# Mixer: seven products of values of cubics for each square or triangle of four filter blocks, and a table for the remainder's taps

## The chip, the cores and the metric

The kernel runs on one NeuronCore of a Trainium2 chip. Five engines work beside each other, each on its own list of instructions in order: PE (TensorE) multiplies matrices into PSUM, DVE (VectorE), ACT (ScalarE) and POOL (GpSimd) do elementwise work, and SP (SyncE) issues DMAs here. They wait for one another by semaphores. The metric is the time of one execution on the device in microseconds (us).

## The reference

Four layers follow one another on an image of 2 x 56 x 56 tokens with 128 channels: two layers of selective scans, then attention plus a spectral mixer, then attention plus a mixture of experts. The change lies in the mixer of the third layer alone. Cut to what matters, it computes this from the layer-normed tokens `u` (2 x 3136 x 128), 16 filters `phi`, and `s = sigma ** 0.25`:

```python
# U_plus: causal convolution of u with each phi[:, k]
# U_minus: the same with u's sign alternating in time, and the sign put back after
out = einsum('btkd,k,kde->bte', U_plus, s, M_phi_plus)
out = out + einsum('btkd,k,kde->bte', U_minus, s, M_phi_minus)
out = out + sum(einsum('btd,de->bte', shifted(u, i), M_u[i]) for i in range(3))
```

It does so for the first T, T/2, T/4 and T/8 tokens with four sets of matrices, and adds the four with the weights of a softmax. The convolution is causal, so the four can share it: which matrices apply depends only on the stretch in which an output token lies.

## The kernel before

Alternating the sign of `u` in time only changes the sign of products between an even and an odd position. So the kernel splits tokens and taps into even and odd ones, of length `HL` = 1568, convolves each parity of the input (`pin`) with each parity of the taps (`eo`), and uses the sum or the difference of the two matrices (`both`) afterwards. A convolution is a lower triangular Toeplitz matrix in blocks of `KB` = 128: `NB` = 12 blocks and a rest of `REST` = 32.

`mixer_filters` prepares the taps. It loads the padded filters into `P`, writes them to DRAM as `raw`, forms 23 sums of blocks of filters on DVE (L1480), and writes them to DRAM as `win`. It runs inside the start of the third layer's attention (`Attention2.run`), and DVE's next instruction after it is the `skip` matrix of the attention (L1286), which its first scores need. During the attention `MixerInputs` lays out the tokens: even ones into the SBUF tile `x`, odd ones through small tiles `r` (two buffers) into the DRAM tile `odd`.

`layer2_mixer` is one stage of 32 units: the parity of the input is the outer loop, then pairs of filters `f0`, then `eo`. Two units with the same pair of filters are called a pair here. In a unit, `H` and the windows `wA` to `wD` hold the Toeplitz matrices, loaded by SP a unit or more ahead. The twelve output blocks are three groups of four: `u0` (a triangle of taps on the first blocks), the two halves of `u1`, and a shared part `S`. The tables `TRIANGLE` and `SQUARE` name each product: which blocks of filters are summed, which combination of inputs stands against it, and to which output blocks it is added. A triangle takes 8 products, a square 9.

`product` (matmuls at L1690) makes one product as 128x256 matmuls for each of two batches, into one of six PSUM buffers `cv`. `into` takes it out: ACT copies the first one for a block (L1705), DVE adds the others to their blocks (L1703), and the sum of S and D (L1707). POOL adds `S` to the second half of `u1` (L1734). `project` multiplies a finished tile with the matrices `Wm` (L1804, two PSUM buffers `pj`), and DVE adds to the output `A` (L1810). `remainder` (L1752) does the last 32 positions for both parities of taps, in units with eo=0.

The order of every engine is the order in which the program is written: `u0`, then the projection of the last unit's `u1` and rest (`finish`), the two halves of `u1`, `S`, `D`, the projection of `u0`, the remainder. Once per pair `matrices` loads `mpm` for two filters, POOL forms `both` (L1784, L1785), DVE the weighted sums `Wm` (L1838, L1840 in `stretch_sums`). Once per parity `inputs` forms the combinations of inputs on DVE (L1619 and the lines after it). Elsewhere, L1840 also serves `MixerInputs`, and L1049 is POOL's end of the second layer.

Of the kernel before, what the change touches and what calls it, by code (L numbers as in the profile page):

```python
# [14 lines left out]
F32 = mybir.dt.float32  # L15
# [6 lines left out]
B = 2  # L22
HW = 56
L = HW * HW
C = 128
# [1384 lines left out]
def key_tiles(k, ps, uT, V, c):  # L1410
# [26 lines left out]
TRIANGLE = (  # L1437
    ((0,), "t3", (3,)), ((3,), "x0", (3,)), ((1,), "t2", (2,)), ((2,), "t1", (1,)), ((0,), "x0", (0,)),
    ((0, 1), "x2", (3, 2)), ((0, 2), "x1", (3, 1)), ((1, 2), "x0", (2, 1)),
)  # L1440
SQUARE = (
    ((0,), "a0", (3,)), ((1,), "a1", (2,)), ((2,), "h0", (1,)), ((3,), "h1", (0,)),
    ((0, 1), "a01", (3, 2)), ((2, 3), "h01", (1, 0)), ((0, 2), "m0", (3, 1)), ((1, 3), "m1", (2, 0)),
    ((0, 1, 2, 3), "m01", (3, 2, 1, 0)),
)


def filter_sums():


    def sums(table, *bases):
        return [tuple(sorted(b + i for i in f for b in bases)) for f, _, _ in table if len(f) * len(bases) > 1]

    first = sums(SQUARE, 0) + [(1, 2)]
    return {"A": first, "B": sums(TRIANGLE, 8), "C": sums(SQUARE, 0, 4), "D": sums(SQUARE, 4)}


SUMS = filter_sums()
NWIN = sum(len(v) for v in SUMS.values())
# [3 lines left out]
def mixer_filters(k, d, dp):  # L1463


    nc = k.nc
    raw = dp.tile([32, PW], F32, name="raw")
    win = dp.tile([32, NWIN, WIDE], F32, name="win")
    with k.tc.tile_pool(name="m2f", bufs=1) as fp:
        P = fp.tile([32, PW], F32, name="P")  # L1470
        nc.gpsimd.memset(P, 0.0)
        nc.sync.dma_start(P[:, KB - TP : KB + HL], d["L2_phi"].rearrange("f p m -> (f p) m"))
        nc.sync.dma_start(raw, P)
        D = fp.tile([32, NWIN, WIDE], F32, name="D")
        done = {(i,): P[:, KB * i + 1 : KB * i + 1 + WIDE] for i in range(NB)}
        at = 0
        for group in SUMS.values():
            for f in sorted(group, key=len):
                two = next((a, b) for a in done for b in done if tuple(sorted(a + b)) == f)
                nc.vector.tensor_tensor(D[:, at + group.index(f)], done[two[0]], done[two[1]], ALU.add)  # L1480
                done[f] = D[:, at + group.index(f)]
            at += len(group)
        nc.sync.dma_start(win, D)
    return raw, win
# [105 lines left out]
class Mixer:  # L1590
# [5 lines left out]

    def __init__(self, k, ctx, given, raw, win):
        self.k, self.x, self.odd, self.raw, self.win = k, given.x, given.odd, raw, win  # L1600
        sp = ctx.enter_context(k.pool("mixv", 1))
        self.wp = ctx.enter_context(k.pool("mixw", 1))
        self.cp = ctx.enter_context(k.pool("mixc", 1))
        self.p1 = ctx.enter_context(k.pool("pconv", 6, psum=True))
        self.sp = sp
        self.H = self.wp.tile([KB, 2, 2, HL], F32, name="H")
        self.W, self.waiting = {}, None

    def inputs(self, par):

        nc, x = self.k.nc, self.x
        if par:
            for j in (8, 4, 0, NB):
                js = slice(j, min(j + 4, NB + 1)) if j == NB else slice(j, j + 4)
                nc.sync.dma_start(x[:, js], self.odd[:, js])
        self.v = {f"x{i}": x[:, NB - 1 - i, :] for i in range(NB)}

        def less(out, a, b):
            nc.vector.tensor_tensor(out, a, b, ALU.subtract)  # L1619

        t = self.sp.tile([KB, 3, B * C], F32, name="t")
        x0, x1, x2, x3 = (self.v[f"x{i}"] for i in range(4))
        nc.vector.scalar_tensor_tensor(t[:, 0], x1, -1.0, x0, ALU.mult, ALU.subtract)
        less(t[:, 1], x1, x2)
        less(t[:, 1], t[:, 1], x0)
        less(t[:, 2], x3, x2)
        less(t[:, 2], t[:, 2], x1)
        self.v |= {f"t{i + 1}": t[:, i] for i in range(3)}

        def twice(v):  # L1630
            return v.unsqueeze(1).to_broadcast([KB, 2, B * C])

        for name in "ACD":

            c = self.scratch("S", 7)
            e = self.scratch("u0", 5)
            v = self.sp.tile([KB, 9, B * C], F32, name="v" + name)
            if name == "A":
                less(c, x[:, 0:7], x[:, 4:11])
            elif name == "C":  # L1640
                c = x[:, 4:11]
            else:
                less(c[:, 0:4], x[:, 8:12], x[:, 4:8])
                nc.vector.tensor_scalar_mul(c[:, 4:7], x[:, 8:11], -1.0)
            less(e, c[:, 0:5], c[:, 2:7])
            less(v[:, 0:2], e[:, 0:3:2], twice(e[:, 1]))
            less(v[:, 2:4], twice(e[:, 3]), e[:, 2:5:2])
            less(v[:, 4:6], c[:, 1:6:4], twice(c[:, 3]))
            less(v[:, 6:8], c[:, 2:5:2], twice(c[:, 3]))
            nc.vector.tensor_copy(v[:, 8], c[:, 3])  # L1650
            self.v |= {name + n: v[:, i] for i, n in enumerate(("a0", "a1", "h0", "h1", "a01", "h01", "m0", "m1", "m01"))}

    def scratch(self, name, n):
        t = self.cp.tile([128, B, 2, 4 * KB], F32, name=name).rearrange("p b f c -> p (b f c)")
        return t[:, 0 : n * B * C].rearrange("p (k c) -> p k c", c=B * C)

    def taps(self, f0, eo):

        self.k.nc.sync.dma_start(
            self.H[:, eo],  # L1660
            bass.AP(self.raw.tensor, self.raw.offset + (2 * f0 + eo) * PW + 1, [[1, KB], [2 * PW, 2], [1, HL]]),
        )

    def windows(self, name, f0, eo):
        n, n0 = len(SUMS[name]), sum(len(SUMS[m]) for m in SUMS if m < name)
# [8 lines left out]
    def products(self, table, name, bases, prefix, eo):  # L1674

        by = {}
        for f, v, outs in table:
            key = tuple(sorted(b + i for i in f for b in bases))
            if len(key) == 1:
                h = self.H[:, eo, :, KB * key[0] : KB * (key[0] + 1)]  # L1680
            else:
                h = self.W[name][:, :, SUMS[name].index(key), :]
            by.setdefault(outs, []).append((self.v[prefix + v], h))
        return by

    def product(self, terms):
        ps = self.p1.tile([128, B, 2, KB], F32, name="cv")
        for b in range(B):
            for i, (v, h) in enumerate(terms):
                self.k.nc.tensor.matmul(  # L1690
                    ps[:, b], lhsT=v[:, C * b : C * (b + 1)], rhs=h, start=i == 0, stop=i == len(terms) - 1
# [3 lines left out]
    def into(self, by, place, onto=None):  # L1695
# [3 lines left out]
        for outs in sorted(by, key=len):  # L1699
            ps = self.product(by[outs])  # L1700
            for o in outs:
                if len(outs) > 1:
                    nc.vector.tensor_tensor(place(o), place(o), ps, ALU.add)  # L1703
                elif onto is None:
                    nc.scalar.copy(place(o), ps)  # L1705
                else:
# [468 lines left out]
```

## Time and profile before

| | us |
|---|---|
| median of three runs | 9005.99 (9002.64 to 9015.55) |
| the profiled execution | 9012.54 |
| its span | 9010.8, mean granted TensorE clock 0.954 |
| scan layers, start of the attention | 0 to 5757 |
| `mixer_filters` and start of the attention proper | 5757 to 5780 |
| attention of layer 3 | 5780 to 6390 |
| mixer | 6400.4 to 8069.3 |
| last attention and experts | 8069.3 to 9010 |

Stages are read from the timeline by the lines that belong to them. In the mixer PE is busy for 1652 of 1669 us, DVE for 1141, ACT for 230 and POOL for 230. In the views below, a row of windows gives for a stretch of time the busy us of each engine with the number of instructions, then the granted clock, the share of DMA and GB/s. A row of waits names who waited, for whom, the total, the number and the longest. A row of a group or a line gives the operation, its shape, the count and the duration, and for a source view the smallest, median and largest duration in ns.

### The profile page before, as it was taken

What the parts mean: (1) busy time and instruction counts of PE and PEld (TensorE: products, weight loads), DVE (VectorE), ACT (ScalarE), POOL (GpSimd) and SP (SyncE); (2) the same over time, 40 slices, a digit from 0 to 9 for tenths busy, and PEclk for the clock granted to TensorE, in tenths of its full rate; (3) what the DMA queues carried; (4) which work ended last, traced back from release to release, by engine and by line L of the source; (5) the groups of instructions that cost most, each with busy time, mean ns of one, the idle gap of its engine ahead of it and who ended that gap; (6) DMA issues with size and microseconds to landing.
All of it is one profiled execution on the core that took longest, in us unless ns stands there. A gap on an engine that the chain in (4) does not pass through costs nothing. (4 is left out here: it accounts for less than half of the span.)

```text
span 9010.8 us, 104738 instructions
## 1 busy us (share of the span) xinstructions
PE 8222.8 (91%) x32399; PEld 5096.0 (57%) x32399; DVE 6874.5 (76%) x7312; ACT 5097.6 (57%) x11031; POOL 6021.1 (67%) x3874
## 2 busy tenths in 40 slices
PE   8999989999998888888888888699999999999998
PEld 4555555555554444444445444455688888874555
DVE  8999988999978996997998899421576676665442
ACT  6888877888866775775776777443211111114331
POOL 5999987999977996996998799466311111115551
PEclk9999999999998997998998999799999999999999
DMA  5666654666645873884785687000333333320004
GB/s 149 217 218 212 212 165 148 217 215 212 211 145 156 223 215 108 227 219 114 217 220 150 179 221 214 10 3 3 91 106 99 103 96 105 94 62 8 15 1 136
DMA packets 751756, 1286.57 MB, mean 143 GB/s; under 512 B 129005, under 2 KB 401390, under 8 KB 751162
## 3 DMA queue, kind: packets, MB, share of 16 engines
q1 hardware_dynamic: 751194, 1279.86, 48.6%
q8 instruction: 257, 4.21, 0.2%
q14 instruction: 305, 2.50, 0.1%
HBM read 1239.96 MB, written 39.60 MB: 142 GB/s over the span
## 5 line engine op out<-in xcount | busy, mean ns | idle before, releaser
L492 POOL TENSOR_TENSOR p<-h,c 128x784 f32<-128x784 f32 x2048 | 3763.8, 1863 | 293.8 <-DVE h L401 147.7
L401 DVE TENSOR_TENSOR_SCAN h<-a,state,h 128x784 f32<-128x784 f32 x1200 | 2169.4, 1832 | 2.9 <-ACT a L381 2.3
L421 PE MATMUL acc<-p,center 128*128 128x392 f32 x4096 | 1491.6, 500 | 6.0 <-POOL p L492 5.9
L421 PE MATMUL acc<-p,ident 128*128 128x392 f32 x4096 | 1431.0, 493 | 0.5 <-POOL p L492 0.4
L476 DVE TENSOR_TENSOR h<-du,b 128x784 f32<-128x784 f32 x1152 | 1095.4, 951 | 233.1 <-PE b L407 211.2
L381 ACT ACTIVATE a<-delta,L1A 128x784 f32<-128x784 f32 x896 | 819.8, 915 | 423.4 <-DVE h L401 418.8
L421 PEld LDWEIGHTS acc<-p,ident 128*128 128x128 f32 x4096 | 748.4, 190 | 534.2 <-issue 34.5
L421 PEld LDWEIGHTS acc<-p,center 128*128 128x128 f32 x4096 | 741.8, 193 | 495.3 <-issue 23.5
L1220 POOL TENSOR_TENSOR total<-total,e 128x448 f32<-128x448 f32 (+1 forms) x644 | 734.2, 1140 | 328.8 <-ACT e L1209 289.2
L1703 DVE TENSOR_TENSOR u<-u,cv 128x512 f32<-128x512 f32 x1024 | 623.2, 678 | 326.7 <-PE cv L1690 325.5
L1734 POOL TENSOR_TENSOR u<-u,S 128x1024 f32<-128x1024 f32 x64 | 150.0, 2364 | 1041.2 <-DVE S L1703 1025.8
L495 POOL TENSOR_TENSOR h<-du,b 128x784 f32<-128x784 f32 x448 | 831.7, 1856 | 0.0
L1209 ACT ACTIVATE e<-sc 128x448 f32<-128x448 f32 (+1 forms) x700 | 376.9, 542 | 726.3 <-PE sc L1207 594.1
L407 PE MATMUL b<-three,sel 96*128 96x512 bf16 (+1 forms) x2304 | 587.5, 336 | 181.4 <-DVE h L476 110.2
L381 ACT ACTIVATE a<-delta,L0A 128x784 f32<-128x784 f32 x704 | 643.2, 914 | 170.3 <-DVE h L401 165.6
L401 DVE TENSOR_TENSOR_SCAN h<-a,h 128x784 f32<-128x784 f32 x400 | 702.4, 1773 | 3.4 <-ACT a L381 3.1
L359 ACT ACTIVATE X<-X,BT 112x128 f32<-112x128 f32 x2100 | 683.8, 391 | 0.2
L1705 ACT COPY u<-cv 128x512 f32<-128x512 f32 x256 | 149.3, 586 | 828.2 <-PE cv L1690 774.6
L401 DVE TENSOR_TENSOR_SCAN h<-h,state,a 128x784 f32<-128x784 f32 x336 | 617.6, 1838 | 0.0
L407 PEld LDWEIGHTS <-sel 96*128 96x128 bf16 x2304 | 224.2, 100 | 526.7 <-issue 367.0
L359 ACT ACTIVATE big<-big,BT 112x64 f32<-112x64 f32 x1680 | 444.6, 335 | 0.0
L370 PE MATMUL a<-ident,X 112*128 112x112 f32 x2240 | 292.7, 269 | 83.5 <-DVE h L401 76.2
(485 smaller groups left out, 13801.3 us busy)
## 6 DMA issues: line engine op xcount, KB each, us to landing
c<-rows SPq DMA_DIRECT2D x1024, 392.0 KB, 4.0
c<-rows SPq DMA_DIRECT2D x2048, 196.0 KB, 4.0
b<-rows SPq DMA_DIRECT2D x512, 196.0 KB, 4.4
b<-rows SPq DMA_DIRECT2D x192, 392.0 KB, 4.5
H<-raw SPq DMA_DIRECT2D x32, 1568.0 KB, 6.4
wC<-win SPq DMA_DIRECT2D x64, 576.0 KB, 5.7
w<-in_L_weight_dram SPq DMA_DIRECT2D x52, 512.0 KB, 4.6
wA<-win SPq DMA_DIRECT2D x64, 384.0 KB, 5.4
```

Of the source, the lines that this page charges most:

```text
L359: self.k.nc.scalar.activation(x["bT"][:, i, c0:c1], g["duT"][x["ci"]][:, i, c0:c1], AF.Copy, scale=g["BT"][:, r : r + 1])
L370: self.k.nc.tensor.transpose(x["b"][:, TP * i : TP * (i + 1)], x["bT"][:, i, :], self.k.ident[:TP, :TP])
L381: self.k.nc.scalar.activation(x["a"], g["delta"][ci], AF.Exp, scale=self.w["A"](g["kd"], ci, x["n"]))
L401: self.k.nc.vector.tensor_tensor_scan(h, a, b, start, ALU.mult, ALU.add)
L407: self.k.nc.tensor.matmul(ps[:, c0:c1], lhsT=self.w["selB"](x["n"]), rhs=x["g"]["three"][:, c0:c1], start=True, stop=True)
L421: nc.tensor.matmul(job["acc"][:, i, 0:392], lhsT=self.w["sum"], rhs=x["p"][:, 392 * i : 392 * (i + 1)], start=False, stop=n == NS - 1,)
L476: nc.vector.tensor_tensor(one["h"], one["g"]["du"][one["ci"]], one["b"], ALU.mult)
L492: nc.gpsimd.tensor_tensor(now["p"], now["h"], now["c"], ALU.mult)
L495: nc.gpsimd.tensor_tensor(three["h"], three["g"]["du"][three["ci"]], three["b"], ALU.mult)
L1209: nc.scalar.activation(e[:n], ps[:n], AF.Exp, scale=scale)
L1220: nc.gpsimd.tensor_tensor(total[:n], total[:n], e[:n], ALU.add)
L1703: nc.vector.tensor_tensor(place(o), place(o), ps, ALU.add)
```

## The change

Each square of four by four blocks is now computed as the product of two polynomials of degree three in disguise: filters and inputs are evaluated at seven points (-1, 1, -2, 2, one half, 0 and infinity), one product is made at each, and the four output blocks are put together from the seven. A triangle is a square with zeros for the missing inputs. There are four sets of filters (A, B, C and D), so 28 values of filters instead of 23 sums, and four sets of inputs (T, A, C, D).

- `mixer_filters` computes the 28 values with 84 DVE operations, and writes them set by set into `win`. It also writes a new DRAM table `last` by 32 DMAs from `raw`, which holds only the taps that the remainder needs; `H` is filled from it and is read by the remainder alone.
- `square` takes the place of `into`. Per square ACT makes two scaled copies (`less`) and `T4`, DVE ten operations with a PSUM operand, six of them scalar_tensor_tensor, and POOL two additions of half a block tile each.
- `unit` makes u0, u2, S and D in this order, each a tile of its own; POOL then adds S to u2 and to u1. Of the waiting projections, u2 and rest come after u0's square, u1 after u2's.
- `inputs` works by set: T and A ahead of a parity's first unit (for the second parity between S and D of the unit before it), C and D inside its first unit. Its scratch tiles are those of the squares. `fetch` loads the odd tokens before the last unit of the first parity.
- `matrices` for the next pair is called in the eo=1 unit between S and the projection of u0; before it stood ahead of the eo=0 unit.

```diff
-TRIANGLE = (
-    ((0,), "t3", (3,)), ((3,), "x0", (3,)), ((1,), "t2", (2,)), ((2,), "t1", (1,)), ((0,), "x0", (0,)),
-    ((0, 1), "x2", (3, 2)), ((0, 2), "x1", (3, 1)), ((1, 2), "x0", (2, 1)),
-)
-SQUARE = (
-    ((0,), "a0", (3,)), ((1,), "a1", (2,)), ((2,), "h0", (1,)), ((3,), "h1", (0,)),
-    ((0, 1), "a01", (3, 2)), ((2, 3), "h01", (1, 0)), ((0, 2), "m0", (3, 1)), ((1, 3), "m1", (2, 0)),
-    ((0, 1, 2, 3), "m01", (3, 2, 1, 0)),
-)
...
+POINTS = ("-1", "1", "-2", "2", "half", "0", "inf")
+SETS = {"A": (0,), "B": (8,), "C": (0, 4), "D": (4,)}
+NWIN = len(POINTS) * len(SETS)
...
+    last = dp.tile([32, KB, NB + 1, REST], F32, name="last")
...
-        D = fp.tile([32, NWIN, WIDE], F32, name="D")
-        done = {(i,): P[:, KB * i + 1 : KB * i + 1 + WIDE] for i in range(NB)}
-        at = 0
-        for group in SUMS.values():
-            for f in sorted(group, key=len):
-                two = next((a, b) for a in done for b in done if tuple(sorted(a + b)) == f)
-                nc.vector.tensor_tensor(D[:, at + group.index(f)], done[two[0]], done[two[1]], ALU.add)
-                done[f] = D[:, at + group.index(f)]
-            at += len(group)
-        nc.sync.dma_start(win, D)
-    return raw, win
+        v = nc.vector
+        for g, bases in enumerate(SETS.values()):
+            D = fp.tile([32, len(POINTS), WIDE], F32, name=f"D{g % 2}")
+            h = [P[:, KB * (bases[0] + i) + 1 : KB * (bases[0] + i) + 1 + WIDE] for i in range(4)]
+            if len(bases) > 1:
+                both = fp.tile([32, 4, WIDE], F32, name="both")
+                for i in range(4):
+                    at = KB * (bases[1] + i) + 1
+                    v.tensor_tensor(both[:, i], h[i], P[:, at : at + WIDE], ALU.add)
+                h = [both[:, i] for i in range(4)]
+            even, odd = (fp.tile([32, WIDE], F32, name=n) for n in ("even", "odd"))
+            for p, (m1, m2) in enumerate(((1 / 9, -1 / 3), (-1 / 60, 1 / 36))):
+                v.scalar_tensor_tensor(even, h[2], float(4**p), h[0], ALU.mult, ALU.add)
+                v.scalar_tensor_tensor(odd, h[3], float(4**p), h[1], ALU.mult, ALU.add)
+                v.tensor_scalar_mul(odd, odd, float(2**p))
+                for q, (m, op) in enumerate(((m1, ALU.subtract), (m2, ALU.add))):
+                    v.tensor_tensor(D[:, 2 * p + q], even, odd, op)
+                    v.tensor_scalar_mul(D[:, 2 * p + q], D[:, 2 * p + q], m)
+            v.scalar_tensor_tensor(even, h[1], 0.5, h[0], ALU.mult, ALU.add)
+            v.scalar_tensor_tensor(odd, h[3], 0.5, h[2], ALU.mult, ALU.add)
+            v.scalar_tensor_tensor(even, odd, 0.25, even, ALU.mult, ALU.add)
+            v.tensor_scalar_mul(D[:, 4], even, 32 / 45)
+            v.tensor_scalar_mul(D[:, 5], h[0], -0.5)
+            v.tensor_copy(D[:, 6], h[3])
+            nc.sync.dma_start(win[:, len(POINTS) * g : len(POINTS) * (g + 1)], D)
+    for f in range(32):
+        nc.sync.dma_start(
+            last[f], bass.AP(raw.tensor, raw.offset + f * PW + 1, [[1, KB], [KB, NB + 1], [1, REST]])
+        )
...
+    def fetch(self):
+
+        for j in (8, 4, 0, NB):
+            js = slice(j, min(j + 4, NB + 1))
+            self.k.nc.sync.dma_start(self.x[:, js], self.odd[:, js])
+
...
+        if name == "C":
+            c = x[:, 4:11]
+        else:
+            c = self.scratch("u0" if name == "D" else "u1", 7)
+            if name == "T":
+                nc.scalar.copy(at(c, 0, 4), x[:, 8:12])
+                nc.gpsimd.memset(at(c, 4, 3), 0.0)
+            elif name == "A":
+                nc.gpsimd.tensor_tensor(c, x[:, 0:7], x[:, 4:11], ALU.subtract)
             else:
+                nc.gpsimd.tensor_tensor(at(c, 0, 4), x[:, 8:12], x[:, 4:8], ALU.subtract)
+                nc.scalar.activation(at(c, 4, 3), x[:, 8:11], AF.Copy, scale=-1.0)
+        v = self.sp.tile([KB, len(POINTS), n], F32, name="v" + name)
+        e = at(v, 0, 6)
+        f, g = self.scratch("T4", 4), self.scratch("T", 2)
+        stt, tt = nc.vector.scalar_tensor_tensor, nc.vector.tensor_tensor
+        stt(e, at(c, 0, 6), -0.5, at(c, 1, 6), ALU.mult, ALU.add)
+        stt(f, at(e, 0, 4), -4.0, at(e, 2, 4), ALU.mult, ALU.add)
+        tt(g, at(e, 3, 2), at(e, 1, 2), ALU.subtract)
+        tt(v[:, 0], f[:, 2], f[:, 1], ALU.subtract)
+        tt(v[:, 1], f[:, 2], f[:, 1], ALU.add)
+        stt(v[:, 2], g[:, 0], -2.0, g[:, 1], ALU.mult, ALU.add)
+        stt(v[:, 3], g[:, 0], 2.0, g[:, 1], ALU.mult, ALU.add)
+        stt(v[:, 4], c[:, 3], -5.0, c[:, 5], ALU.mult, ALU.add)
+        stt(v[:, 4], c[:, 1], 4.0, v[:, 4], ALU.mult, ALU.add)
+        tt(at(v, 5, 2), at(f, 2, 2), at(f, 0, 2), ALU.subtract)
+        self.v[name] = v
...
     def taps(self, f0, eo):
+        n = KB * (NB + 1) * REST
         self.k.nc.sync.dma_start(
             self.H[:, eo],
-            bass.AP(self.raw.tensor, self.raw.offset + (2 * f0 + eo) * PW + 1, [[1, KB], [2 * PW, 2], [1, HL]]),
+            bass.AP(
+                self.last.tensor, self.last.offset + (2 * f0 + eo) * n,
+                [[(NB + 1) * REST, KB], [2 * n, 2], [1, (NB + 1) * REST]],
+            ),
         )
     def windows(self, name, f0, eo):
-        n, n0 = len(SUMS[name]), sum(len(SUMS[m]) for m in SUMS if m < name)
+        n, n0 = len(POINTS), len(POINTS) * list(SETS).index(name)
         t = self.wp.tile([KB, 2, n, KB], F32, name="w" + name)
         for f in range(2):
             r = (2 * (f0 + f) + eo) * NWIN + n0
...
             )
         self.W[name] = t
...
+    def product(self, p, pairs):
         ps = self.p1.tile([128, B, 2, KB], F32, name="cv")
         for b in range(B):
+            for i, (v, w) in enumerate(pairs):
                 self.k.nc.tensor.matmul(
+                    ps[:, b], lhsT=self.v[v][:, p, C * b : C * (b + 1)], rhs=self.W[w][:, :, p, :],
+                    start=i == 0, stop=i == len(pairs) - 1,
                 )
         return ps
+    def square(self, u, *pairs):
         nc = self.k.nc
+        tt, stt = nc.vector.tensor_tensor, nc.vector.scalar_tensor_tensor
+        def y(i):
+            return u[:, :, :, KB * (3 - i) : KB * (4 - i)]
+        T = self.half("T")
+        def t(i):
+            return T[:, :, :, KB * (1 - i) : KB * (2 - i)]
+        for j in range(2):
+            turned = self.tp.tile([128, B, 2, KB], F32, name="less")
+            nc.scalar.activation(turned, self.product(2 * j, pairs), AF.Copy, scale=float(1 + j))
+            ps = self.product(2 * j + 1, pairs)
+            if j == 0:
+                tt(y(2), ps, turned, ALU.add)
+                tt(y(1), ps, turned, ALU.subtract)
+            else:
+                stt(t(0), turned, 0.5, ps, ALU.mult, ALU.add)
+                stt(t(1), ps, 2.0, turned, ALU.mult, ALU.subtract)
+        ps = self.product(4, pairs)
+        for o, share in ((t(0), -0.25), (t(1), -0.125), (y(2), 1.25), (y(1), 0.625)):
+            stt(o, ps, share, o, ALU.mult, ALU.add)
+        T4 = self.half("T4")
+        nc.scalar.activation(T4, T, AF.Copy, scale=4.0)
+        tt(y(0), self.product(5, pairs), y(2), ALU.add)
+        tt(y(3), self.product(6, pairs), y(1), ALU.add)
+        for o, half in ((slice(2 * KB, 4 * KB), T), (slice(0, 2 * KB), T4)):
+            nc.gpsimd.tensor_tensor(u[:, :, :, o], u[:, :, :, o], half, ALU.add)
+    def unit(self, f0, eo, after, later, project, ready, coming):
         nc = self.k.nc
+        u0 = self.block("u0")
+        self.square(u0, ("T", "A"))
+        self.finish(1)
+        u2 = self.block("u2")
+        self.square(u2, ("A", "A"), ("T", "B"))
         if after:
             self.windows("A", *after)
             self.windows("B", *after)
+        self.finish()
+        if ready:
+            self.inputs("C")
+        S = self.block("S")
+        self.square(S, ("C", "C"))
         if after:
             self.windows("C", *after)
+        nc.gpsimd.tensor_tensor(u2, u2, S, ALU.add)
+        coming()
+        project(u0, 0)
+        if ready:
+            self.inputs("D")
+        u1 = self.block("u1")
+        self.square(u1, ("D", "D"))
         if after:
             self.windows("D", *after)
+        nc.gpsimd.tensor_tensor(u1, u1, S, ALU.add)
         if eo == 0:
             self.remainder()
         if later is not None:
             self.taps(later, eo)
         rest = self.rest[:, :, eo]
+        self.waiting = [(u2, 8 * KB), (rest, NB * KB), (u1, 4 * KB)]
+        self.project = project
...
+        Ws = [matrices(f) for f in range(2)]
         for n, (pin, f0, eo) in enumerate(units):
-            if eo == 0:
-                if f0 == 0:
-                    mixer.inputs(pin)
-                Ws = [matrices(f0 + f) for f in range(2)]
+            given = []
+
+            def coming():
+                if eo == 1 and n + 1 < len(units):
+                    if f0 == NF - 2:
+                        mixer.inputs("T")
+                        mixer.inputs("A")
+                    given.extend(matrices((f0 + 2) % NF + f) for f in range(2))
+
+            if (f0, eo) == (NF - 2, 1) and pin == 0:
+                mixer.fetch()
             mixer.unit(
                 f0, eo, units[n + 1][1:] if n + 1 < len(units) else None,
                 units[n + 2][1] if n + 2 < len(units) else None, project(Ws, eo, pin ^ eo),
+                (f0, eo) == (0, 0), coming,
             )
+            Ws = given or Ws
```

## The prediction, as it was put on record before the changed kernel had run

> **What bounds the kernel now.** I read the page first (the share of each engine in 40 slices: from slice 29 to 35 PE is at 9 while DVE falls to 5 to 7), then windows inside the mixer stage: a stretch of 200 us in mid-stage, one unit with eo=1 and the unit with eo=0 after it.
>
> ```profile
> core 0: us, PE busy (x) PEld busy (x) DVE busy (x) ACT busy (x) POOL busy (x), PEclk, DMA share, GB/s
> 6600.00:6800.00 200.00, 200.00 (x992) 173.52 (x992) 134.27 (x232) 28.84 (x50) 27.30 (x16) 1.00 0.34 99
> 6968.00:7016.40 48.40, 48.40 (x230) 41.63 (x229) 29.62 (x51) 7.39 (x13) 4.69 (x2) 1.00 0.40 124
> 7016.40:7070.70 54.30, 54.30 (x282) 47.53 (x282) 40.14 (x70) 7.03 (x12) 9.68 (x6) 1.00 0.31 81
> ```
>
> PE is busy all the time at clock 1.00; DVE 67%, ACT and POOL 14%. A pair of units is 102.7 us, all PE. Then PE's waits between 6390 and 8065:
>
> ```profile
> PE cv L1690 <- ACT u L1705: 7.2, 1, 7.2
> PE pj L1804 <- DVE A L1810: 5.7, 2, 2.8
> PE cv L1690 <- DVE u L1703: 3.0, 1, 3.0
> PE cv L1690 <- DMA H<-raw: 2.5, 1, 2.5
> ```
>
> Some 20 us in 1,669, all at the first unit, the change of parity and the end; in between, none. So matmuls that go away are time, as long as the other engines keep up. PE's timeline prices one:
>
> ```profile
> 7045.81 7.93 PE L1690 MATMUL cv<-wC,vC 128*128 128x256 f32 x36
> 7053.59 3.62 PE L1690 MATMUL cv<-H,vD 128*128 128x256 f32 x16
> ```
>
> 36 records from 7045.81 to 7053.59: 0.216 us each, two records to a matmul.
>
> The groups and source views price the rest. L1703 is DVE's add of a PSUM product, L1734 POOL's add of S, L1705 ACT's copy from PSUM, L1840 the weighted sum with two inputs in SBUF.
>
> ```profile
> L1703 DVE TENSOR_TENSOR u<-u,cv 128x512 f32<-128x512 f32 x1024 | 623.2, 678 | 326.7 <-PE cv L1690 325.5
> L1734 POOL TENSOR_TENSOR u<-u,S 128x1024 f32<-128x1024 f32 x64 | 150.0, 2364 | 1041.2 <-DVE S L1703 1025.8
> L1705 ACT COPY u<-cv 128x512 f32<-128x512 f32 x256 | 149.3, 586 | 828.2 <-PE cv L1690 774.6
> L1703 DVE TENSOR_TENSOR u<-u,cv x1024: 675/677/689, 6408.4 to 8059.1; 128x512 f32<-128x512 f32 x171
> L1840 DVE SCALAR_TENSOR_TENSOR Wm<-both,ws,Wm x96: 475/485/488, 6420.5 to 7873.4; 128x256 f32<-128x256 f32 x96
> L1840 DVE SCALAR_TENSOR_TENSOR wu<-mu,wt,wu x3: 608/611/2722, 5723.3 to 5726.7; 128x384 f32<-128x384 f32 x3
> ```
>
> The last line holds the reason for most of what follows: 611 ns becomes 2,722 once. DVE's timeline beside POOL's shows when:
>
> ```profile
> 5726.08 3.37 DVE L1840 SCALAR_TENSOR_TENSOR wu<-mu,wt,wu 128x384 f32<-128x384 f32 x2
> 5726.69 2.34 POOL L1049 TENSOR_TENSOR X<-X,L1final_ln_w 112x1024 f32<-112x1024 f32 x1 [8.88 <-ACT X L89]
> ```
>
> A DVE instruction with two SBUF inputs that comes up while POOL runs a tensor_tensor stands until POOL is done (2.34 left, plus its own time). L1703, with one input in PSUM, doesn't: its largest is 689 among 1,024, many beside L1734.
>
> **The change part by part**, against the profiled 9012.5 us (span 9010.8), which is 6.5 above the median of 9006.0.
>
> *a. Fewer products.* Convolution records per unit: before 172 (16 + 34 + 18 + 18 = 86 matmuls), after 140 (14 + 28 + 14 + 14 = 70 matmuls). Projections (48 records) and the remainder (52 every second unit) stay. The instruction list of PE has 512 matmuls fewer, 16 a unit. 32 × 0.216 = 6.91 us a unit, 32 units: −221 us. A pair's PE work is then 102.7 − 13.8 = 88.9 us.
>
> *b. Recombination in the steady pair.* Per square ACT makes two scaled copies (0.586 each) and T4 (about 1.05: 112x1024 activations take that); DVE makes 10 operations 128x512 with one PSUM input; POOL makes two adds of 2.36. DVE's pitch back to back is 0.605 (12 in 7.25 us), so a unit has 40 × 0.605 = 24.2 us plus projection adds: less than the 44 us of PE. POOL has 8 × 2.36 + 2 × 4.7 = 28.4 us instead of 4.7. No engine's sum passes PE's; the order decides. By a timetable in the engines' written order, with these durations, 0.1 us a hand-over, six PSUM buffers for products and two for projections: DVE's Wm sums for the next filters (two SBUF inputs; six of 0.485 in each eo=1 unit) now stand between the projection adds, where POOL's halves run. Three or four of them wait up to 2.36 each, so DVE is some 7 us behind PE by square D. In eo=1 nothing like the remainder follows D; the next unit's first product needs a buffer that DVE has not read, and PE waits 4.8 us in two pieces, then 1.7 around the projection of rest. 6.5 us a pair × 16: +104. With no blocking the table gives 2.3 a pair or less (+37); with DVE's scalar_tensor_tensor (STT) at 0.75 instead of 0.605, 9.7 (+155). I take 6.5: no row shows an L1840-type operation passing a POOL add; for an STT with PSUM the nearest rows are STT and TT of 256 elements, both in SBUF, 414 and 417 ns: alike.
>
> *b'. The clock after waits.* The granted clock in a window after a wait:
>
> ```profile
> 6428.50:6432.50 4.00, 3.93 (x10) 2.85 (x11) 4.00 (x8) 0.72 (x2) 2.17 (x2) 0.57 1.00 243
> 7242.80:7246.20 3.40, 3.40 (x6) 2.17 (x7) 3.40 (x7) 1.40 (x3) 0.00 (x0) 0.50 0.00 0
> ```
>
> These follow waits of 2.99 and 7.22 us. Of three waits of 2.8 to 3.0, two were followed by 3.41 us at half clock, one by none. So 16 × 2/3 × 1.7 = +18, between 0 and 16 × 3.4 = 54. The Trainium skill, "TensorE: Matmul & The Clock Gate", Part 1: The HAM clock gate, asks for at least one idle window of about 3.4 us. By that rule waits of 3 to 5 rarely cover a whole window, and this part would be some +6 (an estimate from that page); the two rows after 2.8 and 3.0 us speak against it here.
>
> *c. First unit.* Its inputs: per set 10 DVE operations with two SBUF inputs on 5,120 elements; by (611 − 485)/128 = 0.98 ns an element and some 0.13 each, about 6.4 us. T must come before the first matmul (+6). C and D stand inside unit (0,0), their scratch held by POOL's halves of the square before; PE waits about 9 for C, 11 for D and 5 for A, less the 6 of waits there now: +25 (10 to 35).
>
> *d. Change of parity.* T and A (12.8 us of DVE; 1,792 elements on POOL, 4.1 by L1734's 2.36 for 1,024; POOL's halves, which block them) come between the projection of u0 and D of the last unit: about 23 us of waits; then 3 for A, 5 for C, 11.5 for D in the next. 42.5, less 10.7 before and the 6.5 of the normal pair: +25 (10 to 40). The fetch of x from odd moves from the head of the new parity to before the last unit of the old, where it waits for the remainder to release x; behind it on SP's queue stand only that unit's window loads, needed a unit later. The loads of mpm come a pair early, with DMA at 0.35: both at nothing, and without that unit of lead each would cost the 5 us of a load.
>
> *e. End.* After D, POOL has two halves and u1+=S (9.4 us) before PE's last projection, part of it beside u2's projection: +4.
>
> *f. Filter table.* 84 DVE operations 32x255 instead of 23. Now: 405 ns, pitch 0.335, 7.8 us. After: 44 × 0.335 + 40 × about 0.28 (the row of L1838 is 353 at 256) = 26 us. What follows on DVE is the skip of attention; ACT waited 9.1 us for this DVE line and then 3.5 for the DMA of the table, which is now four smaller ones. Attention2 is PE bound, so a late start carries through. 18 more less 3: +15 (10 to 28).
>
> *g. The copies to `last`.* 32 DMAs DRAM to DRAM, 1,664 elements of 128 bytes: 53,248 packets, ahead of odd<-r on SP's queue. Small packets in the trace took 13 ns: 43 us over 16 engines, done before the first odd<-r at 5836. I cost them at 0; the cover is the 70 us of attention before that. If a packet took 60 ns, 200 us, and the r tiles (two buffers) would hold PE for about 60. H itself shrinks from 1568 to 416 KB a load: hidden before, hidden after.
>
> Sum: −221 + 104 + 18 + 25 + 25 + 4 + 15 = −30. On the profiled run 8982; on the median's basis 8976, and I say 8975.
>
> **The rivals.**
>
> *B: DVE keeps up.* If the Wm sums slip into gaps of POOL, b is 37 and b' near 0: −221 + 37 + 25 + 25 + 4 + 15 = −115, about 8891. For it: DVE's sum is 60% of PE's. Against: the block seen at L1840.
>
> *C, slower: DVE's operation with a PSUM operand and a scalar is longer than the add.* No row shows that form. Twenty-four of a unit's 40 are of it. Break-even for b is 221 − 87 = 134, or 8.4 us a pair, which the table reaches at 0.69 us each. At 0.80: 11.1 a pair, 16 × 11.1 = 178, so +44 net: 9050. Against: STT and TT alike at 256 elements.
>
> *D: the copies to `last` hold SP's queue.* +60: about 9036. Against: 13 ns a packet; for it: no row shows copies of DRAM to DRAM of 128 bytes.
>
> *E: the change doesn't do what it says.* PE's instruction list has the 512 matmuls fewer and the same projections; excluded.
>
> **How the numbers follow.** My forecast (8935 to 9005): 0.45. B: 0.22. C: 0.16. D: 0.08. The rest, larger stalls at the seams (c and d at their upper ends, half clock after every wait): 0.09, about 9010. 0.2% of 9006 is 18 us: faster means under 8988. That holds B and most of mine (0.36 of 0.45): 0.58. Same (8988 to 9024): 0.09 of mine, 0.06 of the seams, 0.04 of C and D: 0.19. Slower: 0.23. The range leaves a tenth at each end: 8875 (B with c and d low) to 9045 (C at 0.79).
>
> **What would show it.** Right: in a mid-stage window PE 93 to 95% busy instead of 100, a pair about 95 us; PE's waits led by a product on DVE, in each pair, 3 to 5 us, just after D of an eo=1 unit; Wm lines whose largest is 2.5 to 2.9 us; DVE's new PSUM rows at 0.68. Wrong: PE still 100% (B); DVE at 100% with rows of 0.8 or more (C); a wait of r or x on odd (D). Wrong altogether if POOL, at 60 to 65% and feeding every projection, ends up last: then waits name POOL and grow past 5 us.

## The result, and the profile after

The changed kernel took 9002.7 us (median of 12 runs, 8992.9 to 9015.0), the kernel before 9004.0 us beside it (12 runs, 8990.5 to 9015.6). The ratio is 0.9998, with a 95% interval of 0.9989 to 1.0007: no difference that this measurement can tell. The prediction said 8975, and put its highest chance on faster. 512 matmuls are gone, and the time is where it was.

The profiled execution of the changed kernel took 9000.1 us, with a span of 8998.3. Set beside the profiled one of before by stages (starts of the stages' first matmuls on PE's timeline):

| stage | before, us | after, us | difference |
|---|---|---|---|
| scans, to the last transposition of the keys (starts at 5757.8 and 5749.5) | 5757.8 | 5749.5 | −8.3 |
| filter table and attention, to the mixer's first matmul (6400.4 and 6405.7) | 642.6 | 656.2 | +13.6 |
| mixer, to the end of its last projection (8070.6 and 8052.5) | 1670.2 | 1646.8 | −23.4 |
| last attention and experts | 940.2 | 945.8 | +5.6 |

The first row is no effect of the change: not one instruction of the scans differs, and in the profiles of the twelve kernels of this document that start lies anywhere from 5734.6 to 5764.0. (Before the change, matmuls of the next stage start ahead of the mixer's last projection, from 8069.3 on.) The mixer became 23 us shorter instead of the 221 us that the matmuls were worth.

The same stretch of the mixer as before, in the window view (busy us of PE, its weight loads, DVE, ACT and POOL with the number of instructions, then granted clock, DMA share, GB/s), and a window that begins at a remainder:

```profile
core 0: us, PE busy (x) PEld busy (x) DVE busy (x) ACT busy (x) POOL busy (x), PEclk, DMA share, GB/s
6600.00:6800.00 200.00, 184.86 (x902) 160.14 (x901) 141.74 (x209) 36.92 (x51) 121.36 (x48) 0.97 0.34 93
...
6773.80:6779.00 5.20, 5.16 (x27) 5.19 (x28) 4.68 (x8) 1.06 (x1) 1.72 (x3) 0.56 0.45 128
```

PE had been busy for 200 of 200 us at clock 1.00. Now it is idle for 15 of them, and after an idle stretch its clock is near half. DVE's busy time has hardly moved (134 to 142 of 200), POOL's went from 27 to 121. What PE waits for in the mixer:

```profile
PE cv L1771 <- DVE u L1712: 98.5, 13, 7.6
PE cv L1686 <- issue: 24.2, 3, 12.2
PE pj L1823 <- POOL u L1744: 15.6, 2, 13.3
PE cv L1686 <- DVE vC L1641: 8.4, 1, 8.4
PE cv L1686 <- DVE u L1712: 6.0, 2, 5.5
```

The first line is the steady state: 13 times 7.6 us, once in each pair of units except the three that are special (the first of either parity, and the last, which makes no matrices). L1771 is the remainder: it needs the PSUM buffer of D's second product, which DVE's L1712 has still to read. The other lines are the first unit, the change of parity and, with 2.3 us of the third, the end.

DVE's timeline of one pair, from the sums of the weighted matrices (L1869, L1871) to its first operation on D (L1711, L1712):

```profile
6750.28 2.53 DVE L1869 TENSOR_SCALAR Wm<-both,ws 128x256 f32<-128x256 f32 x1 [0.64 <-PE pj L1823]
...
6757.46 0.35 DVE L1869 TENSOR_SCALAR Wm<-both,ws 128x256 f32<-128x256 f32 x1 [1.41 <-POOL both L1804]
...
6763.11 2.26 DVE L1871 SCALAR_TENSOR_TENSOR Wm<-both,ws,Wm 128x256 f32<-128x256 f32 x1
6765.29 0.68 DVE L1829 TENSOR_TENSOR A<-A,pj 128x512 f32<-128x512 f32 x1
6765.89 6.60 DVE L1871 SCALAR_TENSOR_TENSOR Wm<-both,ws,Wm 128x256 f32<-128x256 f32 x2
6772.42 0.68 DVE L1711 TENSOR_TENSOR u<-cv,less 128x512 f32<-128x512 f32 x1
6773.02 0.67 DVE L1712 TENSOR_TENSOR u<-cv,less 128x512 f32<-128x512 f32 x1
```

POOL's timeline of the same stretch:

```profile
6748.01 4.66 POOL L1724 TENSOR_TENSOR u<-u,T 128x1024 f32<-128x1024 f32 x2 [6.84 <-DVE u L1722]
...
6762.74 4.84 POOL L1724 TENSOR_TENSOR S<-S,T 128x1024 f32<-128x1024 f32 x2 [5.31 <-DVE S L1722]
6767.66 4.56 POOL L1744 TENSOR_TENSOR u<-u,S 128x2048 f32<-128x2048 f32 x1
```

And PE's, from D's products to the remainder:

```profile
6760.07 6.22 PE L1686 MATMUL cv<-wD,vD 128*128 128x256 f32 x28
6773.84 8.18 PE L1771 MATMUL cv<-H,x 128*128 128x128 f32 x52 [7.56 <-DVE u L1712]
```

Two sums that need 0.48 us each take 6.60 together: the first stands until POOL's second half of S ends at 6767.6, the second until the addition of S to u2 ends at 6772.2. D's first two products were in PSUM at about 6762; DVE takes them up at 6772.4, ten microseconds late, and PE stands still for 7.56. Then the remainder's 52 records, 5.97 us at full clock, take 8.18.

### The profile page after: what moved, and what is told of

Same layout as the page of the kernel before. It is cut to its first block, busy times and chain, and to the rows that moved or that the text cites. A ratio compares the mean times of both kernels' runs of the same rounds, so it can differ in the third digit from the quotient of the medians.

```text
span 8998.3 us, 102947 instructions
## 1 busy us (share of the span) xinstructions
PE 8056.0 (90%) x31375; PEld 4938.9 (55%) x31375; DVE 6921.5 (77%) x7145; ACT 5162.3 (57%) x11035; POOL 6779.2 (75%) x4136
## 5 line engine op out<-in xcount | busy, mean ns | idle before, releaser
L407 PE MATMUL b<-three,sel 96*128 96x512 bf16 (+1 forms) x2304 | 584.9, 335 | 173.8 <-DVE h L476 102.7
L1724 POOL TENSOR_TENSOR u<-u,T 128x1024 f32<-128x1024 f32 x192 | 448.9, 2359 | 382.7 <-DVE u L1722 382.7
L1708 ACT ACTIVATE less<-cv 128x512 f32<-128x512 f32 x256 | 152.3, 595 | 650.3 <-PE cv L1686 619.9
L1720 ACT ACTIVATE T<-T 128x1024 f32<-128x1024 f32 x128 | 135.4, 1058 | 612.5 <-DVE T L1718 553.0
L1823 PE MATMUL pj<-u,Wm 128*128 128x196 f32 (+8 forms) x1536 | 358.8, 387 | 22.4 <-POOL u L1744 15.6
```

The lines of the kernel that those rows point to most:

```text
L407: self.k.nc.tensor.matmul(ps[:, c0:c1], lhsT=self.w["selB"](x["n"]), rhs=x["g"]["three"][:, c0:c1], start=True, stop=True)
L1724: nc.gpsimd.tensor_tensor(u[:, :, :, o], u[:, :, :, o], half, ALU.add)
L1823: nc.tensor.matmul(ps[:, lo - c0 : hi - c0], lhsT=Ws[f][:, eo, r, :], rhs=u[:, b, f, lo - a0 : hi - a0], start=f == 0, stop=f == 1,)
```

## The experiments

Theory 1: DVE's sums of the matrices come up while POOL adds, stand until it is done, and so DVE reaches D late. The rivals: DVE simply has too many operations there; the PSUM buffers are too few for the new order; what counts is the unit in which the sums stand. Ratios and medians are against runs of the kernel before on the same chip.

### The matrices left out

```diff
-                    given.extend(matrices((f0 + 2) % NF + f) for f in range(2))
+                    given.extend(Ws)
```

> The kernel after the change, but the weighted matrices of the first pair of filters serve all pairs: the loads of mpm, POOL's both and DVE's eight sums a pair are left out after the first pair (so the output is not the mixer's). Theory 1 (DVE's sums come up while POOL adds, stand behind it, and so D is taken out of PSUM late): the wait of the remainder for DVE (13 times 7.6 us) and the half clock after it (about 2 us) are gone, a pair falls from 98.8 to about 89, the whole to about 8860. Rival (six PSUM buffers are too few for the new order, whatever DVE does beside it): a pair stays near 98.8 and the whole near 9000.

8872.9 us in its one run, against 9003.2 for the kernel before. The wait of L1771 is gone from the list of PE's waits, and mid-stage the window reads:

```profile
6600.00:6800.00 200.00, 200.00 (x1000) 174.34 (x999) 132.47 (x219) 41.82 (x57) 123.22 (x45) 1.00 0.36 97
```

PE is full again at clock 1.00, with POOL as busy as it was. So six PSUM buffers are enough for the new order; the matrices are the cause. This run leaves out the loads and POOL's `both` along with DVE's sums, so it doesn't yet say whether it is the sums, nor whether by their number or by their waiting.

### One of POOL's additions left out

```diff
-        nc.gpsimd.tensor_tensor(u2, u2, S, ALU.add)
```

> The kernel after the change without POOL's addition of S to u2 (4.56 us a unit), which leaves out a part of the output; DVE's list is the same. Theory 1 (blocking): the last two sums of a pair, 6.6 us together beside that addition, fall by about 4.5, D starts that much earlier, the remainder waits 3 us instead of 7.6, the whole falls by 15 x 4.5 = 65 to 90 us with the clock, to about 8920. Theory 2 (DVE has simply too many operations between S and D, POOL doesn't matter): the wait stays at 7 to 8 us and the whole within 15 us of 9000.

8923.5 us in its one run. DVE's list is unchanged, and the wait fell from 7.6 to 3.5:

```profile
PE cv L1770 <- DVE u L1712: 44.9, 13, 3.5
```

That settles blocking against load: with the same DVE list, the addition taken away lasted 4.56 us, and each of the 13 waits became 4.1 shorter. The longest sum fell from 4,600 to 2,603 ns.

### The sums where POOL is idle

```diff
-                tt(y(1), ps, turned, ALU.subtract)
+                self.turn = tt(y(1), ps, turned, ALU.subtract)
...
         self.square(u2, ("A", "A"), ("T", "B"))
...
+        with self.k.tc.issue_after(self.turn.ins):
+            coming()
         self.finish()
...
-        coming()
+        inputs_ahead()
         project(u0, 0)
```

`issue_after` queues what is written inside it behind the given instruction on its engine; `inputs_ahead` is the part of `coming` that forms T and A for the next parity and stays where it was.

> All work kept; DVE's eight sums of a pair are queued behind the second operation of u2's square in the unit with eo=1, where POOL is idle for 5 to 7 us and DVE has gaps of 6 us. Theory 1: no sum longer than 1 us but the last two, no wait of the remainder for D, a pair of 89 to 90.5, the whole 8860 to 8885 (15 x 8.5 to 9.5 less). Rival (the sums cost PE the same wherever they stand): a pair near 98 and the whole within 20 us of 9000.

8863.2 us (4 runs), ratio 0.9842 (0.9823 to 0.9862). A pair, from the first product of one eo=0 unit to that of the next, is 6508.27 to 6597.16 = 88.89 us, the 88.9 that the prediction had worked out for PE's work alone. All the work is done; it only stands elsewhere. DVE's timeline there shows the sums at their bare length, except the last two, which meet u2's own halves:

```profile
6659.84 0.34 DVE L1873 TENSOR_SCALAR Wm<-both,ws 128x256 f32<-128x256 f32 x1
6660.22 1.53 DVE L1875 SCALAR_TENSOR_TENSOR Wm<-both,ws,Wm 128x256 f32<-128x256 f32 x3
...
6664.73 0.48 DVE L1875 SCALAR_TENSOR_TENSOR Wm<-both,ws,Wm 128x256 f32<-128x256 f32 x1
...
6668.73 2.96 DVE L1875 SCALAR_TENSOR_TENSOR Wm<-both,ws,Wm 128x256 f32<-128x256 f32 x2
```

### The sums in the unit where the prediction had them

```diff
-        tt(y(3), self.product(6, pairs), y(1), ALU.add)
+        self.turn = tt(y(3), self.product(6, pairs), y(1), ALU.add)
...
         self.finish()
+        done = self.turn.ins
...
-        coming()
+        with self.k.tc.issue_after(done):
+            coming()
```

> All work kept; the sums are queued behind the last operation of u2's square in the unit with eo=1, where the prediction had put them (a unit later than the scheduler does). There they meet the halves of u2's square on POOL (4.7 us), not those of S and the addition of 4.56. Theory 1 (what counts is which POOL additions the sums meet): single sums of 2.3 us again, but over before D; PE waits 0 to 3 us a pair, a pair of 89 to 93, the whole 8865 to 8930. Rival (the unit itself counts, by the remainder that follows D or doesn't): 6.5 us a pair as the prediction's table had it, the whole near 8985.

8905.1 us in its one run, a pair 90.9 us (remainders at 6579.91 and 6670.84). PE's waits are two small ones a pair, 1.5 us together:

```profile
PE cv L1686 <- DVE u L1718: 11.3, 14, 0.8
PE cv L1686 <- DVE S L1718: 10.7, 15, 1.3
```

The unit alone isn't what counts. This placement isn't quite the predicted one (the sums come ahead of S's operations and among the first of them here, not between S and u0's projection), so the predicted 6.5 us for that place stays untested.

### The sums on ACT and POOL

```diff
-            stretch_sums(nc.vector, Wm.rearrange("p f r e -> p r f e"), both, lambda i: ws[:, i, f : f + 1])
+            out = Wm.rearrange("p f r e -> p r f e")
+            nc.scalar.activation(out[:, 3], both[:, 0], AF.Copy, scale=ws[:, 0, f : f + 1])
+            for i in range(1, 4):
+                nc.scalar.activation(both[:, i], both[:, i], AF.Copy, scale=ws[:, i, f : f + 1])
+                nc.gpsimd.tensor_tensor(out[:, 3 - i], both[:, i], out[:, 4 - i], ALU.add)
```

> All work kept, at the scheduler's own place; the sums are made by ACT (products, 8 a pair) and POOL (six additions 128x256, some 0.6 each), so no DVE instruction of the steady pairs has two inputs in SBUF. Theory 1: no wait of the remainder, a pair of 89 to 91, the whole 8865 to 8900. Rival (the sums cost by the place in which they stand, on whatever engine): PE waits 4 us or more a pair, for POOL or ACT, and the whole over 8930.

8888.9 us in its one run, a pair 91.3. The remainder waits 0.28 us; ACT, with 8 more operations a pair, is now late by up to 1.3 us, 12 times. With no DVE instruction that POOL can hold, the loss is gone at the scheduler's own place too.

### The filter table later

```diff
-        done = early()
+        done = []
...
+                if (at, j) == (0, 6):
+                    done.extend(early())
```

> All work kept; the filter table is made after the sixth key tile of the attention's first chunk, not ahead of the attention. If the 28.2 us that PE's scores waited (12.0 before) come from the table's 84 operations, whose tiles share memory with the attention's, 20 to 27 us go: 8976 to 8983. Rival (another wait stands at the same place, or DVE's table delays the diagonal tiles of the first chunk as much): less than 8 us.

8982.5 us (10 runs), ratio 0.9977 (0.9965 to 0.9988): some 19 us less than the change as made. The wait ahead of the attention, as the profile of the changed kernel has it, is gone; a smaller one stands at the end of the first chunk, where DVE's copy is queued behind the table. PE's waits ahead of the attention in the changed kernel:

```profile
PE sc L1207 <- ACT e L1209: 28.2, 1, 28.2
```

The longest of PE's waits in the attention in this run:

```profile
PE pr L1236 <- DVE by L1232: 12.6, 2, 11.9
```

### Without the table `last`

```diff
-    for f in range(32):
-        nc.sync.dma_start(
-            last[f], bass.AP(raw.tensor, raw.offset + f * PW + 1, [[1, KB], [KB, NB + 1], [1, REST]])
-        )
...
+        for f in range(2):
+            self.k.nc.sync.dma_start(
+                self.H[:, eo, f],
+                bass.AP(
+                    self.last.tensor, self.last.offset + (2 * (f0 + f) + eo) * PW + 1,
+                    [[1, KB], [KB, NB + 1], [1, REST]],
+                ),
+            )
```

Here `self.last` is `raw`.

> One part undone, all work kept: no table last and none of its 32 copies (53,248 packets); the remainder's taps come straight from raw, two loads of 1,664 pieces of 128 bytes a unit. If the copies were hidden, as the prediction has it, and the loads are, nothing: within 10 us of 9003. If the copies held up the attention or the odd tokens, 10 to 60 less; if the loads in small pieces come late, PE waits for H and it is more.

9001.8 us (10 runs), ratio 0.9994 (0.9985 to 1.0004). The table costs nothing that can be measured and brings nothing.

### Both remedies, and the table in pieces

The moved sums and the late table in one kernel:

> The moved sums and the late filter table together, all work kept. If the two losses are independent, the gains add: about 140 and 20 us less than the change as made, 8843 (8835 to 8855), some 1.8% under the kernel before the change. If the late table's DVE work or its DMAs collide with something that the moved sums need, less than 150 in all.

8846.6 us (5 runs), ratio 0.9822 (0.9808 to 0.9835). The gains add.

Then the table set by set, one set at the sixth key tile of each chunk; `early` became a generator:

```diff
+                if j == 6:
+                    done.extend(next(parts, ()))
```

> All work kept: the moved sums as in the run with both, and the filter table made set by set, one set at the sixth key tile of each of the attention's first four chunks (some 7 us of DVE each), the copies to last in the fifth. In the run with the whole table in the first chunk, PE waited 11 us at that chunk's end for DVE's copy, which stood behind the table. If that wait is the table's length alone, it goes: 8 to 12 us less than with the whole table, about 8836. If the attention's chunks have no such slack in DVE, or the table's tiles collide with the chunks' own, the waits come back as four short ones and nothing is gained.

8851.0 us (5 runs), ratio 0.9820 (0.9807 to 0.9834): nothing gained. DVE's timeline showed why: all four sets were issued ahead of the end of the first chunk again, since their inputs were ready, and PE's wait was 11.9 us as before. So each piece was held back:

```diff
-            nc.vector.tensor_copy(by, acc)
+            self.mark = nc.vector.tensor_copy(by, acc)
...
+                if at > 0 and j == 6:
+                    with k.tc.issue_after(att.mark.ins):
+                        done.extend(next(parts, ()))
```

> As the run before, but each set's operations are queued on DVE behind the copy that ends the attention's chunk before, since the last trace shows that the scheduler had issued all four sets ahead of the first chunk's end again and PE had waited the same 11.9 us. If that wait is the table's length in one piece, it goes now: 8 to 12 us less than 8847 to 8851, about 8838. If the four pieces cost the same in the four chunks, nothing is gained.

8840.7 us (5 runs), ratio 0.9818 (0.9804 to 0.9831), and the wait of 11.9 is not in the list of PE's waits. This is the fastest version that was run, 1.8% under the kernel before; its step over the version with the whole table in the first chunk (0.9822) lies inside the intervals. In its profile the stretch from the last transposition of the keys to the mixer's first matmul is 6375.85 − 5746.07 = 629.8 us, 12.8 less than before the change.

## Why the prediction was right or wrong

Its range held the time, its direction did not come. The range reached from 131 us under 9006 to 39 above, so that holding 9002.7 says little, and 9002.7 stands at the upper edge of its own forecast, 8935 to 9005. Its signs of being right came, each stronger than predicted: PE was busy for 92% of the mid-stage window (93 to 95 predicted), a pair took 98.8 us (95), the wait on DVE was 7.6 us (3 to 5), the longest sum 4.6 us (2.5 to 2.9). By its steps:

**a, the products: right.** 88.89 us a pair where nothing disturbs it, against 102.7 before and 88.9 predicted.

**b, the recombination: the right mechanism, mis-sized, and put in the wrong unit.** The prediction had 6.5 us of waits a pair; 7.58 were measured (98.5 / 13). It took the sums to stand in the eo=1 unit, where `matrices` is called, and the wait to fall on the next unit's first product. They stand in the eo=0 unit ahead of it, where the buffers of older matrices come free after u1's projection, and so just before the remainder. The sentence in the description of the kernel, that the order of every engine is that in which the program is written, is wrong for this kernel: a scheduler puts an instruction where its inputs and buffers are ready. The run with the table in pieces shows the same. And "three or four of them wait up to 2.36 each" left out the longest: the addition of S to u2 holds one sum for its whole 4.56. The four sums that were held took 2.53 + 2.26 + 6.60 = 11.4 us where 0.35 + 3 × 0.48 = 1.8 is their bare time. That is 9.6 us of standing; with 1.4 of waiting for POOL's `both` it makes 11.0, enough for the ten microseconds by which DVE is late. That 6.5 and 7.58 lie so close is in part luck: the unit was wrong and the longest hold was left out, and with the sums held in the predicted unit, if not quite at the predicted place, PE waited 1.5 us a pair.

**b', the clock: twice the size.** 1.1 us a pair was assumed, and 2.3 came: a pair is 98.80 us (remainders from 6576.71 to 7169.53 over six pairs), and 98.80 − 88.89 − 7.58 = 2.33. This term was mis-sized, not misplaced. The remainders after the waits of 7.6 us took 7.8 to 8.7 us instead of 5.97, in all eleven that the timeline shows whole.

Steady pairs together: 13 × 9.9 = 129 us, where the prediction's terms give 13 × 7.6 = 99.

**c, the first unit: right.** From its first matmul to the next unit's, 80.2 us (6405.72 to 6485.88). Its own work is 39.7: 47.3 of a steady eo=0 unit less the 7.6 us of projections that it doesn't have. So 40.4 of stalls against 7.4 before: +33, predicted 25 and the 7.6 of a normal pair.

**d, the change of parity: right.** From the end of D to the next unit's first product 91.8 us (7219.2 to 7310.95), 44.4 more than the work; before, 10.7 of waits and 3.4 of half clock: +30, predicted 25 on top of the 6.5 of a normal pair.

**e, the end:** what the mixer's −23.4 leaves is 221 − 129 − 33 − 30 − 23.4 = 5.6, predicted 4; the last pair makes no matrices and loses nothing, where the sum had counted a normal pair's 7.6.

**f, the filter table: right.** PE's wait ahead of the attention went from 12.0 to 28.2 us, the stage grew by 13.6; predicted 15. Why: ACT's first exponential waited for DVE's table, 25.4 us instead of 9.1 (and 3.5 for the DMA).

**g, the copies to `last`: right.** They were over by 5809, some 53 us after the first was issued, ahead of the first odd tokens at 5840; nothing waited for them, and without them the time was the same. Rival D falls.

**The rivals.** B, DVE keeping up, did not come about by itself; the runs that move the same work show what it would have been (8863 and, with the table late, 8841 to 8851). C falls by one row, scalar_tensor_tensor with a PSUM operand, against 678 for the plain add beside it (L1721):

```profile
L1718 DVE SCALAR_TENSOR_TENSOR T<-cv,T x256: 671/680/693, 6417.2 to 8034.6; 128x512 f32<-128x512 f32 x128
```

The sum of the profile: −30 predicted, −12 measured, of which −8 are the scans. The remaining 26 are in the main b and b' (30 more in the steady pairs, less the last pair's 7.6) and 5.6 in the stage after the mixer. Nothing in the change touches that stage: in the twelve profiles it takes either 938 to 940 or 945 to 946 us, whatever the kernel does ahead of it, so the 5.6 are no cost of the change. By the medians the change was worth −1.3.

What had been read off the trace, durations and blocking, held. What failed was the place of the sums, taken as the program's text has it, the length of the additions that they meet there (4.56 us where 2.36 was the longest counted), and the size of the half clock (2.3 us a pair where 1.1 was counted).

## What to carry to other kernels

A saving on the bounding engine is worth what the others let through: check not only their sums of busy time (DVE's was 71% of the time) but which of their instructions can be held by which others, and what stands behind those in the queue. Work that is off the critical path but shares DVE's queue and POOL's time belongs where POOL is idle, and with a scheduler it must be held there by a dependency; the place in the program does not hold it. After a wait is costed, add the half clock that follows.

## What the runs showed of the hardware that was not expected

**DVE operations with one tensor input in SBUF are held by POOL as well.** L1869, a tensor_scalar of 128x256, goes from 354 to 2,551 ns; in the run with the late table, tensor_scalar of 32x255 takes 1.21 us instead of 0.27 beside POOL's sums of the attention, while neighbours that begin just ahead of one of these sums take 0.27 and 0.28. DVE's timeline there:

```profile
5753.69 0.27 DVE L1479 TENSOR_SCALAR D<-P 32x255 f32<-32x255 f32 x1
5753.89 1.21 DVE L1471 TENSOR_SCALAR odd<-odd 32x255 f32<-32x255 f32 x1
5755.04 0.28 DVE L1480 COPY D<-P 32x255 f32<-32x255 f32 x1
```

POOL's timeline beside it:

```profile
5753.70 3.87 POOL L1220 TENSOR_TENSOR total<-total,e 128x448 f32<-128x448 f32 x3 [3.72 <-ACT e L1209]
```

Operations with one input in PSUM and one in SBUF were never held: L1718's largest is 693. The Trainium skill, "SBUF — State Buffer", section "Who interferes with whom", counts tensor_scalar and copies among the operations that can take the shared ports. The rows of tensor_scalar agree; of copies, one of 32x255 in the run with the table in pieces took 1.23 us instead of 0.28.

**The holding goes both ways.** POOL's addition of 128x1024 to S has a median of 2,360 ns and a largest of 3,863, in a unit where DVE forms inputs from SBUF: there POOL's two halves of S last from 7284.61 to 7290.77, 6.16 us instead of 4.7, beside an operation of DVE on vD that stands from 7284.70 to 7288.58.

**Half clock after waits.** Waits of 3.46 us (the run without the addition) were followed by remainders of 7.4 to 9.0 us instead of 5.97, in all ten that the timeline shows whole. With waits of at most 0.8 and 1.3 us (the sums in the eo=1 unit) the granted clock stayed at 1.00 from 6600 to 6800. In the run without the addition, a window that begins at such a remainder, and two that lie about the start of another:

```profile
6661.10:6664.60 3.50, 3.45 (x16) 3.48 (x17) 3.50 (x7) 1.06 (x1) 1.34 (x2) 0.50 0.23 68
...
7039.14:7042.55 3.41, 1.04 (x9) 1.08 (x10) 3.38 (x7) 0.00 (x0) 2.48 (x3) 1.00 0.00 0
7042.55:7045.96 3.41, 3.41 (x18) 3.41 (x18) 3.41 (x7) 1.06 (x1) 0.24 (x1) 0.50 0.56 160
```

The Trainium skill, "TensorE: Matmul & The Clock Gate", Part 1: The HAM clock gate, asks for at least one idle window of about 3.4 us, which runs freely; a wait of 3.46 would then seldom contain a whole one. Ten in ten says that a shorter idle time within a window is enough here.

The last two rows show how much. This remainder begins at 7041.51, still at full clock; at 7042.55 the clock falls for 3.41 us, behind a stretch of 3.41 us in which PE was busy for 1.04 and idle for 2.37. In the mixers of the twelve profiles the granted clock changes only at whole multiples of 3.41 us from one another. Counted in such stretches, half clock followed every one in which PE was idle for 1.98 us or more, and none in which it was idle for 1.96 or less; as the ends of PE's records are modelled, the bound is some 2.0 us. This also explains why, before the change, one wait of 2.83 us had no half clock behind it: it was shared by two stretches, with 1.80 us of idle time in the first and 1.71 in the second, a short wait of 0.68 included (7220.40 to 7223.82 and on to 7227.23).
